# Two post-norm layers on one core: the router's transposes of six batches taken off TensorE

## The chip, the cores and the metric

The kernel runs on one core of a Trainium2 chip. The metric is the device time of one execution in microseconds, given as the median of several runs. Besides the times there is one profiled execution of the same program, recorded by the hardware profiler; all durations of single instructions come from it.

## What is computed

Eight batches of 512 tokens, each a row of 512 numbers in f32, go through two layers. Each layer is attention and then a feed-forward part, each of which is added to its input and followed by a layernorm. Cut to what matters:

```python
# layer 0, attention: 16 heads of 32, causal
q, k, v = x @ WQ.T + bq, x @ WK.T + bk, x @ WV.T + bv
attn = softmax(where(causal, -inf, q @ k.T / sqrt(32)))
x = layernorm(x + (attn @ v) @ WO.T + bo)
# layer 0, feed-forward: 8 experts, the best two for each token
logits = x @ (gate_weight + 2 * lora_B @ lora_A).T          # 512 -> 8
w, chosen = top_k(softmax(logits), 2);  w = w / w.sum()
x = layernorm(x + sum(w * expert_e(x) for e in chosen))
# layer 1: attention with 8 heads of 64, then a feed-forward part with integer weights (512 -> 1408 -> 512)
```

The change concerns one step of layer 0: how the rows `x` after the first layernorm are turned (features on the partitions, tokens along the row), so that TensorE can form `logits` from them.

## The kernel before

The whole of layer 0's attention is `attention0` (from L1182). It works batch by batch (b = 0 to 7), in each batch through four groups of four heads (g = 0 to 3), and in each group through three **units** (u = 0, 1, 2), which cover the key tiles 0, then 1 and 3, then 2. A place in this order is written (g, u) here. A unit does the following on TensorE: the scores of its own heads (`scores`, L1324), then whatever other work the plan has put into that place, then the product of the *unit before it* with the values (`product`, L1348), and in the units with u = 1 the row sums of the group before (`normalise`, `rs`, L1363). Between a unit's scores and its product lie ScalarE's exponential (L1328) and GpSimd's causal mask (L1333). VectorE adds up the exponentials (L1356), inverts the row sums (L1366) and scales (L1367).

`plan(b)` (from L1378) writes by hand which other work goes into which place: the values, queries and keys (the query and key of the next group, and those of the next batch's first group at the end), and the late work of the batch before it, pb = b - 1. For pb that work is, in order:

- `project(pb, t)`, four token tiles t: 8 matmul instructions of the output projection (L1276), VectorE adds the residual (L1277) and takes the statistics; after the last tile `layernorm` (L173 to L188) has GpSimd form the reciprocal deviation (L182, L183), VectorE normalise the four tiles (L185) and SyncE's queue write the rows to memory (L188);
- `turn(pb, c)`, four feature chunks c: four transposes on TensorE into one bank of PSUM (L1288) and a copy to `x1T` by VectorE (L194) or ScalarE (L192);
- `score(pb)`: eight matmul instructions give the logits (L491), ScalarE copies them (L1298); `choose(pb)`: four small pairs of matmuls (L503), then some 25 short VectorE instructions, which pick the experts;
- two batches later `dispatch`, `one_hot` and `enter`, which put the tokens into the experts' tables (L547 to L590).

`merge` (L776 to L794) adds a low-rank term to two chunks of the experts' weights: two pairs of matmuls (L781), two ScalarE scalings (L792), two GpSimd additions (L794).

TensorE's results other than scores and products share two PSUM banks (tag `mm`). `x1T` shares one room with the one-hot rows; `aoT`, the attention output, has one room, so that the first group's result of batch b can't be written before pb's last projection has read the old one; `r_inv` and the scaled merge rows share two rooms.

The order in `plan` isn't the final order. Outside of a few stretches marked `in_order`, a planner at build time lists each engine's instructions by its own estimate of when their inputs are ready, with the program's order as priority. Each engine, and SyncE's queue of DMAs, then works through its list strictly in order. So a lower-priority transfer may stand ahead of its place in the program: the input of batch b + 2 (`load_xT`, L1212) is issued in batch b as soon as `key(b, 3)` has read its room.

The class `Turn` (L73 to L104) is in the kernel already and serves the last feed-forward part (`IntegerFfn.blocks`, seven batches). It turns a batch without TensorE: VectorE transposes blocks of 32x32 (L88), four DMAs write each partition quarter's blocks to their place in memory (`out`, L93, 256 KB each), and one DMA of 1 MB reads the turned batch back (`back`, L96). The tokens then stand in the order (block of 32, tile, token), and `by_tile` puts them back into tile order at some later copy.

Of the kernel before, what the change touches and what calls it, by code (L numbers as in the profile page):

```python
# [9 lines left out]
F32 = mybir.dt.float32  # L10
# [8 lines left out]
P = 128  # L19
NB = 8  # L20
S = 512
D = 512
NT = S // P
ND = D // P
# [48 lines left out]
class Turn:  # L73
# [677 lines left out]
class Experts:  # L751
# [430 lines left out]
def attention0(env, guard, keep, routes, experts, dram, p_mm, tiles_ctx):  # L1182
# [4 lines left out]
    tc, nc, ins, xs, vec = env.tc, env.nc, env.ins, env.xs, env.vec  # L1187
# [3 lines left out]
    with ExitStack() as phase:  # L1191
        work = phase.enter_context(tc.tile_pool(name="a_work", bufs=1))
# [54 lines left out]
        def mm(shape, name):  # L1247
            return p_mm.tile(shape, F32, tag="mm", name=name)

        def value(b, t):  # L1250
            ps = mm([P, D], "ps_v")
            for c in range(ND):
                nc.tensor.matmul(ps, lhsT=xts[b][:, c, ts(t, P)], rhs=wv[:, c, :], start=c == 0, stop=c == ND - 1)  # L1253
            vs[t] = own.tile([P, D], F32, tag=f"v{t}", name=f"v{t}")
            nc.vector.tensor_tensor(vs[t], ps, row[:, 0, :], ALU.add)  # L1255

        def query(b, g):
            ps = mm([P, S], "ps_q")
            for c in range(ND):
                nc.tensor.matmul(ps, lhsT=wq[:, g, ts(c, P)], rhs=xts[b][:, c, :], start=c == 0, stop=c == ND - 1)  # L1260
            q = own.tile([P, S], F32, tag="q", name="q", bufs=2)
            nc.vector.tensor_scalar(q, ps, vec[:, V_BQ + g : V_BQ + g + 1], None, ALU.add)
            heads[b, g] = [q]

        def key(b, g):
            ps = mm([P, S], "ps_k")
            for c in range(ND):
                nc.tensor.matmul(ps, lhsT=wk[:, g, ts(c, P)], rhs=xts[b][:, c, :], start=c == 0, stop=c == ND - 1)
# [12 lines left out]
        x1Ts, logits = {}, {}  # L1281

        def turn(b, c):
            if c == 0:
                x1Ts[b] = work.tile([P, ND, S], F32, tag="x1T", name="x1T")
            ps = mm([P, S], "ps_x1T")
            for t in range(NT):
                nc.tensor.transpose(ps[:, ts(t, P)], xs[b][:, t, ts(c, P)], env.ident)  # L1288
            if b == NB - 2:
                nc.scalar.copy(x1Ts[b][:, c, :], ps)  # L1290
            else:
                env.evacuate(c, x1Ts[b][:, c, :], ps)

        def score(b):
            ps = mm([P, S], "ps_logits")
            router.logits(x1Ts.pop(b), ps)
            logits[b] = work.tile([P, S], F32, tag="logits", name="logits")
            nc.scalar.copy(logits[b], ps)  # L1298

        def choose(b):  # L1300
# [7 lines left out]
        def one_hot(b, places):  # L1308
            if places[0] == 0:
                rooms[b] = work.tile([P, ND, S], F32, tag="x1T", name="one_hot")  # L1310
            return router.one_hot(b, rooms[b], places)

        def enter(rows):
            router.enter(mm([P, 2, E * E_TILES], "ps_table"), *rows)

        def scores(b, g, u):
            q, k = heads[b, g]
            sc = p_sc.tile([P, 4, S], F32, tag="sc", name="sc")
            width = 0
            for kt in UNITS[u]:  # L1320
                w = S - P * kt
                for j in range(4):
                    hs = slice(HD * j, HD * (j + 1))
                    nc.tensor.matmul(sc[:, j, width : width + w], lhsT=k[hs, ts(kt, P)], rhs=q[hs, P * kt :],  # L1324
                                     start=True, stop=True)
                width += w
            p = own.tile([P, 4, width], F32, tag=f"p{u}", name="p", bufs=2 if u == 0 else 1)
            nc.scalar.activation(p, sc[:, :, :width], AF.Exp, scale=scale)  # L1328
# [49 lines left out]
        def plan(b):  # L1378

            todo = {(g, u): [] for g in range(ND) for u in range(len(UNITS))}  # L1380
            for slot, places in (((0, 0), (0, 1)), ((0, 1), (3,)), ((0, 2), (2,))):
                todo[slot] += [lambda t=t: value(b, t) for t in places]
            for g in range(ND):
                nb, ng = (b, g + 1) if g + 1 < ND else (b + 1, 0)
                if nb < NB:
                    todo[g, 1].append(lambda nb=nb, ng=ng: query(nb, ng))
                    todo[g, 2].append(lambda nb=nb, ng=ng: key(nb, ng))
            pb, last = b - 1, b == NB - 1
            if b:
                places = ((1, 0), (1, 0), (1, 1), (1, 1) if last else (1, 2))  # L1390
                for t, slot in enumerate(places):
                    todo[slot].append(lambda t=t: project(pb, t))
                places = ((2, 0),) * 4 if last else ((2, 1), (2, 1), (2, 2), (2, 2))
                for c, slot in enumerate(places):
                    todo[slot].append(lambda c=c: turn(pb, c))
                todo[(2, 1) if last else (3, 0)].append(lambda: score(pb))
                todo[(2, 2) if last else (3, 1)].append(lambda: choose(pb))
                if not last:
                    todo[2, 0].append(merge)
                    todo[3, 0].append(merge)  # L1400
# [34 lines left out]
        for b in range(NB):  # L1435
            todo = plan(b)
            for g in range(ND):
# [16 lines left out]
                for u in range(len(UNITS)):  # L1454
                    p = scores(b, g, u)
# [15 lines left out]
        b = NB - 1  # L1471
# [627 lines left out]
```

## Time and profile before

| | us |
|---|---|
| median of three runs (lowest, highest) | 2272.99 (2271.68, 2275.99) |
| the profiled execution's own time | 2270.12 |
| its span, first to last instruction | 2268.4 |
| TensorE busy in the span | 2224.5 |
| VectorE, ScalarE, GpSimd busy | 1257.6, 645.4, 494.5 |
| one batch of layer 0's attention, three stretches of 93, 94, 93 us: TensorE busy | 92.4, 92.8, 91.9 |
| the same: VectorE busy | 47.7, 60.9, 59.0 |

The span is cut into stages that follow one another: layer 0's attention to about 750 us, its experts to about 1210 us, layer 1's attention to about 1763 us and its feed-forward part to the end. A line of the timeline gives the start, the length, the engine, the line of the kernel, the operation, what it writes and reads, the tile shape, how many instructions were merged into it, and in brackets the idle time before it and what ended that. One f32 product of TensorE is two matmul instructions in these lines. The granted clock of TensorE is full (0.996) in the mean.

### The profile page before, as it was taken

The numbers are of one execution on the slowest core, as the hardware profiler recorded it, in microseconds if no ns is written. First come the engines' busy times: TensorE is split into PE (matmuls) and PEld (weight loads), VectorE is DVE, ScalarE is ACT, GpSimd is POOL, SyncE is SP. The second block draws the span as 40 slices with busy tenths as digits, with TensorE's granted clock in tenths as the row PEclk, the third lists the DMA queues.
The fourth block names the chain that finished last, engine by engine and source line by source line (L and its number), as shares of the span: only waits on it lengthen the run. The fifth ranks groups of instructions, "written<-read, shape, count | busy, mean of one in ns | idle before, by whom it ended". The sixth has DMA issues, their size and how long they took to land. (4 is left out here: it accounts for less than half of the span.)

```text
span 2268.4 us, 24071 instructions
## 1 busy us (share of the span) xinstructions
PE 2224.5 (98%) x9318; PEld 1142.3 (50%) x9318; DVE 1257.6 (55%) x2004; ACT 645.4 (28%) x937; POOL 494.5 (22%) x489
## 2 busy tenths in 40 slices
PE   9999999999999999999999999999999999999997
PEld 3344444444444444444453333433443778888876
DVE  3557676575767443242216776787666654445443
ACT  2332323323233221111124333332332222222222
POOL 2332423313223341131105223312211000000000
PEclk9999999999999999999999999999999999999999
DMA  8010101101022225242214111101100331111000
GB/s 292 19 56 1 56 19 38 57 1 56 28 64 75 93 66 194 88 125 88 89 58 160 34 56 56 47 10 47 38 0 1 103 93 56 56 56 46 29 19 20
DMA packets 74236, 141.31 MB, mean 62 GB/s; under 512 B 6770, under 2 KB 21106, under 8 KB 73218
## 3 DMA queue, kind: packets, MB, share of 16 engines
q1 hardware_dynamic: 62832, 104.01, 13.6%
q0 software_dynamic: 10560, 34.61, 5.4%
q8 instruction: 76, 1.25, 0.2%
q10 hardware_dynamic: 722, 1.07, 0.1%
q14 instruction: 46, 0.38, 0.1%
HBM read 96.93 MB, written 42.73 MB: 62 GB/s over the span
## 5 line engine op out<-in xcount | busy, mean ns | idle before, releaser
L877 PE MATMUL ps_gu<-experts,xrT 128*128 128x512 f32 (+1 forms) x520 | 247.1, 598 | 0.0
L1328 ACT ACTIVATE p<-sc 128x2048 f32<-128x2048 f32 (+1 forms) x96 | 152.9, 1592 | 189.0 <-PE sc L1324 182.2
L1333 POOL TENSOR_SCALAR_AFFINE_SELECT p<-p 128x512 f32<-128x512 f32 x128 | 91.8, 731 | 381.7 <-ACT p L1328 378.2
L1116 DVE SCALAR_TENSOR_TENSOR hT<-ps_u,vec,sg 128x512 f32<-128x512 f32 x88 | 65.5, 745 | 195.3 <-PE ps_u L1111 195.3
L1127 PE MATMUL ps_f<-ffn_w,h_half 128*128 128x512 f32 x672 | 170.3, 393 | 0.6 <-issue 0.4
L966 POOL TENSOR_TENSOR g_total<-g_total,r_inv 128x512 f32<-128x512 f32 x64 | 89.6, 1401 | 359.5 <-DVE r_inv L1677 283.5
L1677 DVE RECIPROCAL r_inv<-r_inv 128x512 f32<-128x512 f32 x32 | 106.9, 3339 | 97.6 <-ACT r_inv L963 97.6
L1647 ACT ACTIVATE p<-sc 128x1024 f32<-128x1024 f32 x128 | 124.0, 1021 | 125.9 <-PE sc L1644 125.9
L1356 DVE TENSOR_TENSOR p<-p 128x1536 f32<-128x1536 f32 (+2 forms) x96 | 129.1, 1345 | 39.5 <-POOL p L1333 22.5
L1127 PEld LDWEIGHTS ps_f<-ffn_w,h_half 128*128 128x128 f32 x672 | 124.4, 188 | 33.0 <-DVE h_half L1122 5.5
L880 DVE TENSOR_TENSOR h<-ps_gu,h 128x256 f32<-128x256 f32 x67 | 28.3, 423 | 202.5 <-ACT h L879 202.5
L1111 PE MATMUL ps_g<-x_high,ffn_w 128*128 128x512 f32 x352 | 138.9, 395 | 0.8 <-DVE x L1618 0.8
L1111 PE MATMUL ps_g<-x_low,ffn_w 128*128 128x512 f32 x352 | 139.0, 395 | 0.0
L1111 PE MATMUL ps_u<-x_low,ffn_w 128*128 128x512 f32 x352 | 138.7, 394 | 0.0
L1111 PE MATMUL ps_u<-x_high,ffn_w 128*128 128x512 f32 x352 | 138.7, 394 | 0.0
L894 PE MATMUL ps_y<-experts,hT 128*128 128x512 f32 (+1 forms) x272 | 127.9, 593 | 0.5 <-ACT hT L888 0.5
L1644 PE MATMUL sc<-qT,kT 64*128 64x512 f32 x512 | 127.3, 615 | 1.0 <-ACT qT L1565 0.7
L1260 PE MATMUL ps_q<-experts 128*128 128x512 f32 x256 | 121.1, 615 | 4.4 <-DMA experts<-in_xT 4.4
L1666 PE MATMUL av<-p,v 128*64 128x512 f32 x512 | 123.8, 605 | 0.0
L877 PEld LDWEIGHTS ps_gu<-experts,xrT 128*128 128x128 f32 x520 | 89.2, 191 | 67.6 <-issue 67.6
L1253 PE MATMUL ps_v<-experts 128*128 128x512 f32 x256 | 116.3, 602 | 3.2 <-DVE v L1255 3.2
L1612 PE MATMUL ps_o<-attn_out,aoT 128*128 128x512 f32 x256 | 117.3, 602 | 0.8 <-ACT r_inv L963 0.8
(259 smaller groups left out, 3521.5 us busy)
## 6 DMA issues: line engine op xcount, KB each, us to landing
results<-y SPq DMA_DIRECT2D x68, 256.0 KB, 2.0
x<-in_x SPq DMA_DIRECT2D x8, 1024.0 KB, 7.7
experts<-in_gate_up SPq DMA_DIRECT2D x8, 1024.0 KB, 10.7
rows<-x SPq DMA_DIRECT2D x32, 256.0 KB, 2.0
x<-rows SPq DMA_DIRECT2D x8, 1024.0 KB, 10.9
experts<-in_xT SPq DMA_DIRECT2D x7, 1024.0 KB, 5.4
turned<-turned SPq DMA_DIRECT2D x28, 256.0 KB, 3.9
turned<-turned SPq DMA_DIRECT2D x7, 1024.0 KB, 4.8
```

The source lines that it names most:

```text
L877: mm = nc.tensor.matmul(ps, lhsT=xT[:, c, :], rhs=self.weights(i, c), start=c == 0, stop=c == ND - 1)
L894: self.nc.tensor.matmul(ps, lhsT=hT[:, c, :], rhs=self.weights(i, ND + c), start=c == 0, stop=c == self.NI - 1)
L1111: nc.tensor.matmul(ps, lhsT=w[:, ts(dc, P)], rhs=x[:, dc, :], start=(dc, i) == (0, 0), stop=(dc, i) == (ND - 1, 1))
L1127: self.nc.tensor.matmul(os[t], lhsT=h[:, ts(t, P)], rhs=self.weights(2 * NHID + c), start=(c, i) == (0, 0), stop=(c, i) == (NHID - 1, 1))
L1253: nc.tensor.matmul(ps, lhsT=xts[b][:, c, ts(t, P)], rhs=wv[:, c, :], start=c == 0, stop=c == ND - 1)
L1260: nc.tensor.matmul(ps, lhsT=wq[:, g, ts(c, P)], rhs=xts[b][:, c, :], start=c == 0, stop=c == ND - 1)
L1328: nc.scalar.activation(p, sc[:, :, :width], AF.Exp, scale=scale)
L1356: nc.vector.tensor_tensor(total[:, :, P * kt :], total[:, :, P * kt :], p[:, :, at : at + w], ALU.add)
L1612: nc.tensor.matmul(ps, lhsT=state[b]["aoT"][:, c, ts(t, P)], rhs=w_out[:, c, :], start=c == 0, stop=c == ND - 1)
L1644: nc.tensor.matmul(sc[:, j, :], lhsT=st["kT"][hs, ts(kt, P)], rhs=st["qT"][g][hs, :], start=True, stop=True)
L1647: nc.scalar.activation(p, sc, AF.Exp, scale=scale)
L1666: nc.tensor.matmul(st["av"][HD * j : HD * (j + 1), :], lhsT=st["v"][:, kt, HD * j : HD * (j + 1)], rhs=p[:, j, :], start=kt == 0, stop=kt ...
```

## The change

For the batches 0 to 5 the four `turn` calls are replaced by one `blocks(b)`: four VectorE block transposes, four DMAs out and one back, with a new `Turn` and its own DRAM tile. The logits of these batches have their tokens in block order; ScalarE's copy to `logits` reads and writes through `by_tile` and restores tile order. The batches 6 and 7 are turned on TensorE as before.

While such a batch is the batch before (b = 1 to 6), the plan of b is another:

| place | before | after |
|---|---|---|
| (1,0) | project 0, 1 | project 0 |
| (1,1) | query, project 2, table | query, project 1, table |
| (1,2) | key, project 3 | key, project 2 |
| (2,0) | merge | project 3 |
| (2,1) | query, turn 0, 1 | query, blocks, merge |
| (2,2) | key, turn 2, 3 | key |
| (3,0) | score, merge | query of the next batch |
| (3,1) | query of the next batch, choose | score, merge |
| (3,2) | key of the next batch | key of the next batch, choose |

```diff
+        by_blocks = NB - 2
+        turns = Turn(env, dram, NT, "turned0")
+
+        def room(b):
+            x1Ts[b] = work.tile([P, ND, S], F32, tag="x1T", name="x1T")
+
+        def blocks(b):
+            room(b)
+            flat = x1Ts[b].rearrange("p k s -> p (k s)")
+            for t in range(NT):
+                turns.blocks(flat, t, xs[b][:, t, :])
+            turns.out(flat)
+            turns.back(flat)
+
...
-            nc.scalar.copy(logits[b], ps)
+            if b < by_blocks:
+                nc.scalar.copy(turns.by_tile(logits[b], False), turns.by_tile(ps, True))
+            else:
+                nc.scalar.copy(logits[b], ps)
...
+            pb, last = b - 1, b == NB - 1
+            by_dma = 0 <= pb < by_blocks
...
-                    todo[g, 1].append(lambda nb=nb, ng=ng: query(nb, ng))
+                    todo[g, 0 if by_dma and ng == 0 else 1].append(lambda nb=nb, ng=ng: query(nb, ng))
...
-                places = ((1, 0), (1, 0), (1, 1), (1, 1) if last else (1, 2))
+                places = ((1, 0), (1, 1), (1, 2), (2, 0)) if by_dma else ((1, 0), (1, 0), (1, 1), (1, 1) if last else (1, 2))
...
-                places = ((2, 0),) * 4 if last else ((2, 1), (2, 1), (2, 2), (2, 2))
-                for c, slot in enumerate(places):
-                    todo[slot].append(lambda c=c: turn(pb, c))
-                todo[(2, 1) if last else (3, 0)].append(lambda: score(pb))
-                todo[(2, 2) if last else (3, 1)].append(lambda: choose(pb))
+                if by_dma:
+                    todo[2, 1].append(lambda: blocks(pb))
+                else:
+                    for c in range(ND):
+                        todo[2, 0].append(lambda c=c: turn(pb, c))
+                todo[(3, 1) if by_dma else (2, 1)].append(lambda: score(pb))
+                todo[(3, 2) if by_dma else (2, 2)].append(lambda: choose(pb))
                 if not last:
-                    todo[2, 0].append(merge)
-                    todo[3, 0].append(merge)
+                    todo[2, 1].append(merge)
+                    todo[3, 1].append(merge)
```

More of the change, by code (lines that the diff above doesn't have):

```diff
@@ L1281, in attention0 @@
         x1Ts, logits = {}, {}
+        by_blocks = NB - 2
[9 more added lines that the diff above has]
+            turns.back(flat)
         def turn(b, c):
             if c == 0:
-                x1Ts[b] = work.tile([P, ND, S], F32, tag="x1T", name="x1T")
+                room(b)
             ps = mm([P, S], "ps_x1T")
@@ L1385, in plan @@
                 if nb < NB:
-                    todo[g, 1].append(lambda nb=nb, ng=ng: query(nb, ng))
+                    todo[g, 0 if by_dma and ng == 0 else 1].append(lambda nb=nb, ng=ng: query(nb, ng))
                     todo[g, 2].append(lambda nb=nb, ng=ng: key(nb, ng))
-            pb, last = b - 1, b == NB - 1
             if b:
-                places = ((1, 0), (1, 0), (1, 1), (1, 1) if last else (1, 2))
+                places = ((1, 0), (1, 1), (1, 2), (2, 0)) if by_dma else ((1, 0), (1, 0), (1, 1), (1, 1) if last else (1, 2))
                 for t, slot in enumerate(places):
                     todo[slot].append(lambda t=t: project(pb, t))
-                places = ((2, 0),) * 4 if last else ((2, 1), (2, 1), (2, 2), (2, 2))
-                for c, slot in enumerate(places):
-                    todo[slot].append(lambda c=c: turn(pb, c))
-                todo[(2, 1) if last else (3, 0)].append(lambda: score(pb))
-                todo[(2, 2) if last else (3, 1)].append(lambda: choose(pb))
+                if by_dma:
[5 more added lines that the diff above has]
+                todo[(3, 2) if by_dma else (2, 2)].append(lambda: choose(pb))
                 if not last:
-                    todo[2, 0].append(merge)
-                    todo[3, 0].append(merge)
+                    todo[2, 1].append(merge)
+                    todo[3, 1].append(merge)
             if b == 0:
```

## The prediction

> **What bounds the kernel now.** I read the busy shares first, then the chain that ended last, then one batch of layer 0 on TensorE's timeline.
>
> ```profile
> PE 2224.5 (98%) x9318; PEld 1142.3 (50%) x9318; DVE 1257.6 (55%) x2004; ACT 645.4 (28%) x937; POOL 494.5 (22%) x489
> ```
>
> TensorE is busy 98% of the span, and the chain that ended last is mostly TensorE, so time taken off TensorE's list is time won, as long as nothing else is late in its place. The two pairs of transposes and their surroundings in batch 4 (places (2,0) to (3,0)) show what they cost; the columns are start, length, line and what was written:
>
> ```profile
> 419.30 1.14 PE L1324 MATMUL sc<-q,k 32*128 32x512 f32 x8
> 420.28 1.03 PE L781 MATMUL ps_lora<-lora 16*128 16x512 f32 x4
> 421.23 0.64 PE L1348 MATMUL av<-p,v 128*32 128x256 f32 x8
> 422.44 1.15 PE L1324 MATMUL sc<-q,k 32*128 32x384 f32 x16 [0.57 <-ACT p L1328]
> 423.52 3.70 PE L1260 MATMUL ps_q<-experts 128*128 128x512 f32 x8
> 427.05 0.60 PE L1288 MATMUL ps_x1T<-ident,x 128*128 128x128 f32 x4
> 427.58 1.04 PE L1348 MATMUL av<-p,v 128*32 128x512 f32 x2
> 428.56 0.66 PE L1288 MATMUL ps_x1T<-ident,x 128*128 128x128 f32 x4
> ...
> 431.00 0.71 PE L1324 MATMUL sc<-q,k 32*128 32x256 f32 x8
> 431.64 3.70 PE L1268 MATMUL ps_k<-experts 128*128 128x512 f32 x8
> 435.18 0.60 PE L1288 MATMUL ps_x1T<-ident,x 128*128 128x128 f32 x4
> 435.71 0.83 PE L1348 MATMUL av<-p,v 128*32 128x384 f32 x2
> 436.47 0.66 PE L1288 MATMUL ps_x1T<-ident,x 128*128 128x128 f32 x4
> ...
> 438.05 1.14 PE L1324 MATMUL sc<-q,k 32*128 32x512 f32 x8
> ```
>
> The reader is to see two things. The transposes stand inside the products (av), of which otherwise four run side by side; two are torn off and run alone (0.98 us for two instructions). And at 422.44 TensorE waits for the exponential, because (2,0) holds almost nothing.
>
> **What goes.** In (2,1), from the end of the query's issue to the next scores: 431.00 - 427.05 = 3.95 us. The same products and row sums without transposes, in (1,1) of this batch, take 410.59 - 408.74 = 1.85. Difference 2.10. In (2,2): 438.05 - 435.18 = 2.87, against 419.30 - 418.30 = 1.00 for the same products in (1,2). Difference 1.87. Together 3.97 a batch. The transposes' own share of it is 0.53 + 0.59 + 0.53 + 0.59 = 2.24. In (2,0) the gap ahead of the scores goes too, since a projection (3.5 us) now stands there and covers the exponential (1.88 us): from 421.23 to 422.44 is 1.21, of which (1,1)'s like product needs 0.57, so 0.64. The rest of the batch, all places from (1,0) to (3,2), lasts 65.07 us (390.14 to 455.21). Its pieces at their undisturbed lengths make 59.7 without transposes: scores, products and row sums 6.2 for each of three groups, six queries and keys at 3.53, four projections at 3.53, table 1.84, logits 1.0, two merges 2.0, choice 0.9. So at most 65.07 - 59.7 = 5.4 us can be won in a batch, and I can place 3.97 + 0.64 = 4.6 of it; the rest is a low-rank pair torn across scores in (3,0).
>
> A rule of the Trainium skill would make the gain larger. The trace has 272 ns as the duration of a transpose, but 0.109 us from one's start to the next. "TensorE: Matmul & The Clock Gate", part 4, gives about 275 ns for a transpose in a kernel; sixteen at that price would be an estimated 4.4 us a batch instead of 2.24. Here the trace agrees with the length and shows that it isn't the price.
>
> **What TensorE gets instead.** The matmuls of the logits, projections, merges and queries are the same ones in other places. New is that a merge in (2,1) needs both banks of tag mm between the query and the row sums, and in (3,1) after the logits. The pairs can be torn as the transposes were. Below: 0. Above: 2.10 in (2,1), the transposes' own price there, and 1.0 in (3,1) (a pair's length). I take 0.7 and 0.4, nearer to nothing, since a merge has two tiles to place and not sixteen instructions.
>
> **The wait that is added.** Logits now wait for VectorE and two rounds of DMA. The prices come from the same class in the last stage and from this stage's norm:
>
> ```profile
> DMA to landing us min/median/max: 3.0/4.1/5.0
> ...
> turned<-turned SPq DMA_DIRECT2D x7, 1024.0 KB, 4.8
> ```
>
> ```profile
> 422.12 4.14 DVE L185 TENSOR_SCALAR x<-x,mv,rstd 128x512 f32<-128x512 f32 x4 [1.48 <-POOL rstd L183]
> ```
>
> From the end of project 3 (418.30) to the first normalised tile's start is 3.8 us (residual, statistics, GpSimd's deviation; 422.12). Four tiles take 4.14 beside GpSimd's mask and merge, but 0.55 each, 2.2, elsewhere; the merge now comes later, so 3.1. The query's copy between them is 0.4 to 0.75, the four block transposes 2.5 (1789.21 to 1791.7 in the last stage, 0.67 each, overlapped). From there the first write is issued, the read back 6.6 us later (1791.72 to 1798.33), and it lands 4.9 us after that (1803.25): 11.5. SyncE's queue holds one more thing: the load of x (1 MB), which is free to go as soon as the blocks are read, and the planner will list it ahead of the read back, which must wait for the writes. Two such loads 1.8 us apart (435.37 and 437.16) landed after 5.4 and 6.7 us, so a load in front costs the one behind it some 1 us; I add 0.7. Sum: 3.8 + 3.1 + 0.4 + 2.5 + 11.5 + 0.7 = 22.0 us.
>
> What covers it: after project 3, TensorE has the product of (2,0) 0.57, then (2,1) scores 1.07, query 3.53, merge 1.0, product and row sums 1.85, then (2,2) 5.2 and (3,0) 5.2 (scores, a key or query of 3.53, products), then (3,1)'s scores 1.07: 19.5, with the torn merge 20.2. So logits stall TensorE for 22.0 - 20.2 = 1.8 us. Behind them in its list stand the merge, the product of (3,0) and the row sums, and ScalarE's logits copy. Would the planner move the logits back? GpSimd's addition to the next x (L1442) waits 3 us for its load in each of five batches (15.3 us in all), ahead of merge work that is ready at 442.0, 4.8 us after the load's issue at 437.16: the planner takes such a load as landed by then, and will believe that logits are ready in time. I take the wait as real. Bounds: none (all lengths at their short end, 20.8, beside a fully torn merge), and 7 us (normalising at 4.14, both 1 MB loads ahead of the read back at 3.3 each, which is what 6.7 + 1.8 - 5.4 says of the second's own transfer).
>
> **What lies beside other work.** VectorE gets four transposes (2.7) and loses two copies (1.35), at 59 of 93 us busy; ScalarE loses two copies. The logits copy with split rows has no row in this stage; between its 0.58 and twice that I take 0.58, since it moves the same 512 numbers a partition, and ScalarE is free. 2 MB more a batch against a DMA share of 10% are covered but for the queueing above. Choice moves from 8 us before the batch's end to the end, so its 25 VectorE instructions meet the next batch's values, where TensorE already waits for the copy of a value (1.39 us at 372.15). Below 0, above 1.4; I take 0.5. The next batch's query in (3,0) has its input long before: its load was issued a batch ahead.
>
> A rule of the skill speaks against the whole change. Here four writes in 512-byte pieces land within 6.5 us (1791.72 to 1798.19). "VectorE: DVE Perf Modes", section "The three transpose paths", calls a plain DMA that transposes by strides 19 times slower than the crossbar's, and its "Rules for kernel authors" leave 128x128 to TensorE; stretched like that, the estimate for a 4.9 us transfer is 90 us, far beyond any cover. The writes here move whole 512-byte runs, which is why I follow the rows.
>
> **The sum.** Per batch 5.4 - 0.7 - 0.4 - 1.8 - 0.5 = 2.0 us won; six batches 12 us. The profiled execution took 2270.1, so 2258; the median of the runs is 2.9 above it, so 2261 from there. I write 2260.
>
> **Rivals.**
> - *The planner places the logits late enough*, behind the merge, product and row sums of (3,1) (2.85 us of work): the stall of 1.8 is covered, and the merge ahead of them isn't torn. 5.4 - 0.7 - 0.5 = 4.2 a batch, 25 us: 2245 to 2248 (by the profiled execution, by the median), so 2246. For it: the planner does reorder by readiness. Against: its early GpSimd add. Chance 0.18.
> - *The road through memory is too long*: the key of (2,2) frees the next input's room at about 433, near the time at which the writes land, and that load, too, goes ahead of the read back. The stall then is about 6 us with slow normalising, and 5.4 - 1.6 - 6 = -2.2 a batch, 13 us more: 2284. It decides from a stall of 4 us on (5.4 - 0.7 - 0.4 - 0.5 is 3.8). For it: the queue is in order, and 11.5 us of its road has no slack. Against: the read back is listed earlier if the planner thinks the writes short. Chance 0.24.
> - *The change does what it says, but the stall and the choice eat the gain* (3 to 4 us): 2270. Chance 0.11.
> - The forecast, 2260: chance 0.47.
>
> **The numbers.** A difference under 0.2% (4.5 us) can't be told from no change in this kernel. The forecast's case is faster but for a small part (0.02 within), so faster 0.63, within 0.13, slower 0.24. The range reaches down to 2242, where nothing is torn and nothing waits but the choice (5.4 - 0.5 = 4.9, six times 29), and up to 2284, the slow rival.
>
> **What would show it.** TensorE at full clock with a batch of 89 to 92 us in place of 93.4; no L1288 in six batches; ahead of L491 a gap for the DMA of x1T of 1 to 3 us, in each of six batches; the read back landing about 12 us after the last block transpose, with x's load issued ahead of it; no gap ahead of the scores after (2,0). I am wrong if that gap is over 4 us, if TensorE stalls on the banks in (2,1) by more than a transpose pair did, or if VectorE runs late at the batch's start.

## The result, and the profile after

The changed kernel takes 2287.7 us (median of six runs, 2282.9 to 2289.2) against 2271.6 for the kernel before (six runs on the same chip, 2267.7 to 2276.0). The ratio is 1.0066, 95% interval 1.0054 to 1.0078: **slower by 16 us**. The forecast was 2260 and faster; its range ended at 2284.

The profiled execution took 2287.86 us, its span is 2286.1. The line of busy times in the page of the changed kernel:

```profile
PE 2237.0 (98%) x9222; PEld 1132.3 (50%) x9222; DVE 1259.6 (55%) x2016; ACT 640.0 (28%) x925; POOL 485.0 (21%) x489
```

The 96 transposes are gone from TensorE (9318 instructions became 9222), and yet TensorE is busy for 12.5 us longer. The mean granted clock fell from 0.996 to 0.989. So what is left got slower or stands more apart; and nearly all of it lies in the stage that was changed: the first write to `results` (start of the experts) moves from 748.66 to 765.41 us, by 16.75 of the 17.7 us that the span grew.

The nearest answer is in batch 4 again, places (2,0) to (3,1), on TensorE's timeline of the changed kernel (start, length, line, what was written, count, and in brackets the wait before it):

```profile
428.56 1.15 PE L1341 MATMUL sc<-q,k 32*128 32x384 f32 x16
429.63 3.70 PE L1260 MATMUL ps_q<-experts 128*128 128x512 f32 x8
433.27 1.12 PE L781 MATMUL ps_lora<-lora 16*128 16x512 f32 x2
434.32 1.04 PE L1365 MATMUL av<-p,v 128*32 128x512 f32 x2
437.45 1.12 PE L781 MATMUL ps_lora<-lora 16*128 16x512 f32 x2 [2.09 <-DVE q L1262]
438.50 0.63 PE L1365 MATMUL av<-p,v 128*32 128x512 f32 x3
...
438.98 2.42 PE L1380 MATMUL rs<-p,ones 128*32 128x512 f32 x7
441.32 1.24 PE L1341 MATMUL sc<-q,k 32*128 32x256 f32 x8
...
452.49 1.15 PE L1341 MATMUL sc<-q,k 32*128 32x384 f32 x16
453.57 1.06 PE L491 MATMUL ps_logits<-x1T,r_wr 128*32 128x512 f32 x8
454.56 1.12 PE L781 MATMUL ps_lora<-lora 16*128 16x512 f32 x2
455.62 1.04 PE L1365 MATMUL av<-p,v 128*32 128x512 f32 x2
456.59 1.12 PE L781 MATMUL ps_lora<-lora 16*128 16x512 f32 x2
```

The gap that was predicted ahead of the logits (L491) isn't there: they start right behind the scores. The gap is in (2,1), at 437.45: the second pair of the merge wants a bank of `mm`, and that bank still holds the query. VectorE's timeline of the same stretch says why:

```profile
431.81 2.56 DVE L185 TENSOR_SCALAR x<-x,mv,rstd 128x512 f32<-128x512 f32 x4 [1.48 <-POOL rstd L183]
434.29 2.48 DVE L88 STREAM_TRANSPOSE x1T<-x 128x512 f32<-128x512 f32 x4
436.69 0.70 DVE L1262 TENSOR_SCALAR q<-ps_q,vec 128x512 f32<-128x512 f32 x1
```

TensorE has issued the last of the query at about 433.2. VectorE's list has four normalisations and four block transposes ahead of its copy, so the copy starts 3.5 us later. The waits of the whole stage name the same pair, in each of the six batches (engine, line, releaser: total us, times, longest):

```profile
PE ps_lora L781 <- DVE q L1262: 12.5, 6, 2.1
```

What comes after the wait costs as much again. The busy times by stretch, TensorE's clock in the third column from the end:

```profile
437.00:439.00 2.00, 1.55 (x10) 0.49 (x13) 0.40 (x1) 0.33 (x1) 0.00 (x0) 1.00 0.43 84
439.00:441.00 2.00, 2.00 (x14) 0.28 (x6) 1.20 (x1) 0.27 (x1) 1.27 (x1) 0.58 0.91 169
441.00:443.00 2.00, 2.00 (x12) 0.91 (x10) 2.00 (x2) 1.06 (x3) 0.00 (x0) 0.57 0.95 220
443.00:445.00 2.00, 2.00 (x6) 0.92 (x5) 2.00 (x1) 0.65 (x1) 0.63 (x1) 1.00 0.96 219
```

At 0.58 and 0.57 over 4 us, the clock was halved for 3.4 us, which loses 1.7 us. Here seven instructions of the row sums last 2.42 us, where eight take 1.04 in place (1,1) of the same batch (413.61). Most of the loss is therefore counted as TensorE busy: in the whole span TensorE is idle for only 5.2 us more than before (49.1 against 43.9).

The queue of DMAs in that batch, from SyncE's timeline (issue, time the issue took, line):

```profile
436.79 3.79 SPq L93 DMA_DIRECT2D turned<-x1T  x4
440.75 1.25 SPq L1216 DMA_DIRECT2D x<-in_x  x1
444.29 0.33 SPq L96 DMA_DIRECT2D x1T<-turned  x1
```

The next x is loaded ahead of the read back, as predicted. From the first write's issue to the read back's it takes 7.5 us; the read back lands 7.6 us later, at 451.9. From the end of the last projection (427.9) the road is 24.0 us long.

The table counts a place from its first score to the next place's, in us, as the mean of the batches 2 to 5. Other places are within 0.1 of each other in all kernels but for (1,0), which is 5.27 with the new plan and 8.70 with the old.

| kernel | (0,0) | (0,1) | (0,2) | (2,0) | (2,1) | (2,2) | (3,0) | (3,1) | (3,2) | batch | median us |
|---|---|---|---|---|---|---|---|---|---|---|---|
| before | 8.70 | 10.68 | 9.07 | 3.14 | 8.56 | 7.06 | 3.69 | 8.20 | 5.28 | 93.5 | 2271.6 |
| after | 8.70 | 10.00 | 9.07 | 5.27 | 13.08 | 6.00 | 5.27 | 7.00 | 6.07 | 96.2 | 2287.7 |
| e1 | 8.83 | 10.00 | 9.07 | 6.32 | 7.41 | 6.70 | 7.92 | 4.19 | 6.07 | 92.2 | 2265.5 |
| e2 | 8.71 | 10.00 | 9.07 | 5.27 | 11.33 | 7.06 | 5.27 | 7.00 | 6.25 | 95.7 | 2288.0 |
| e3 | 8.70 | 10.00 | 9.07 | 5.27 | 8.46 | 5.28 | 5.27 | 14.35 | 6.38 | 98.5 | 2303.1 |
| e4 | 9.49 | 10.00 | 9.07 | 6.32 | 7.41 | 6.70 | 5.27 | 4.75 | 8.29 | 93.0 | 2267.2 |
| e5 | 9.41 | 10.00 | 9.07 | 5.27 | 8.46 | 5.28 | 5.27 | 9.25 | 7.89 | 95.6 | 2284.5 |
| e6 | 12.35 | 10.00 | 9.07 | 6.32 | 7.41 | 5.28 | 7.92 | 3.79 | 6.53 | 94.4 | 2278.1 |
| e7 | 9.54 | 10.00 | 9.07 | 6.32 | 10.13 | 7.06 | 7.92 | 3.79 | 6.07 | 95.6 | 2285.8 |
| e8 | 8.70 | 10.00 | 9.07 | 3.14 | 6.56 | 5.28 | 3.14 | 20.64 | 5.28 | 101.0 | 2314.6 |
| e9 | 9.49 | 10.00 | 9.07 | 6.32 | 7.41 | 7.17 | 5.27 | 11.54 | 5.28 | 97.3 | 2293.8 |
| e11 | 8.70 | 10.00 | 9.07 | 5.27 | 13.18 | 5.91 | 5.27 | 7.00 | 6.07 | 96.2 | 2287.4 |
| e12 | 9.49 | 10.00 | 9.07 | 6.32 | 10.20 | 7.06 | 6.88 | 8.88 | 5.30 | 98.9 | 2308.4 |
| e13 | 9.50 | 10.00 | 10.41 | 6.32 | 7.41 | 7.17 | 5.27 | 3.99 | 5.28 | 91.1 | 2253.8 |
| e14 | 9.49 | 10.00 | 10.41 | 6.32 | 10.20 | 7.06 | 6.88 | 3.99 | 5.28 | 95.3 | 2284.9 |
| e15 | 8.70 | 10.00 | 10.36 | 3.14 | 8.56 | 7.06 | 3.69 | 8.20 | 5.28 | 94.1 | 2274.9 |

After less before is 2.67 us a batch, 16.0 in six: (1,0) -3.4, (2,0) +2.1, (2,1) +4.5, (2,2) -1.1, (3,0) +1.6, (3,1) -1.2, (3,2) +0.8, (0,1) -0.7.

### The profile page after: what moved, and what is told of

It is laid out like the page before. It is cut to its first block, busy times and chain, and to the rows that moved or that the text cites. A ratio compares the mean times of both kernels' runs of the same rounds, so it can differ in the third digit from the quotient of the medians.

```text
span 2286.1 us, 23911 instructions
## 1 busy us (share of the span) xinstructions
PE 2237.0 (98%) x9222; PEld 1132.3 (50%) x9222; DVE 1259.6 (55%) x2016; ACT 640.0 (28%) x925; POOL 485.0 (21%) x489
## 3 DMA queue, kind: packets, MB, share of 16 engines
q10 hardware_dynamic: 722, 1.07, 0.1%
## 5 line engine op out<-in xcount | busy, mean ns | idle before, releaser
L1373 DVE TENSOR_TENSOR p<-p 128x1536 f32<-128x1536 f32 (+2 forms) x96 | 136.3, 1420 | 60.8 <-PE av L1365 59.2
L1350 POOL TENSOR_SCALAR_AFFINE_SELECT p<-p 128x512 f32<-128x512 f32 x128 | 82.7, 658 | 404.9 <-ACT p L1345 338.4
L1268 PE MATMUL ps_k<-experts 128*128 128x512 f32 x256 | 118.3, 605 | 0.2 <-ACT r_inv L963 0.2
## 6 DMA issues: line engine op xcount, KB each, us to landing
experts<-in_gate_up SPq DMA_DIRECT2D x8, 1024.0 KB, 11.3
```

The source lines that it names most:

```text
L1373: nc.vector.tensor_tensor(total[:, :, P * kt :], total[:, :, P * kt :], p[:, :, at : at + w], ALU.add)
```

## The experiments

The first theory was that the place of the merges costs the time: with VectorE late, the merge in (2,1) waits for its bank. The rivals were the road through memory, the choice at the batch's start, and the block copy.

**e1: the merges back in (2,0) and (3,0), all else as changed.**

```diff
-                    todo[2, 1].append(merge)
-                    todo[3, 1].append(merge)
+                    todo[2, 0].append(merge)
+                    todo[3, 0].append(merge)
```

> The changed kernel with its two merges back in (2,0) and (3,0); nothing else moved. Theory A (the loss is the banks: in (2,1) the second merge pair waits for a bank that VectorE empties only after four normalised tiles and four block transposes): no wait of a merge pair for VectorE's query copy is left, (2,1) lasts about 6.5 us instead of 12.8, and if nothing else is short, 4 to 4.5 us a batch are won against the kernel before: about 2246 us. Theory B (the road through memory is too long for the cover, and in the changed kernel the bank wait only hid that): the turned rows land 24 us after project 3's end, as in the changed kernel, but logits come up after 20.5 us; TensorE waits 3 to 4 us for that DMA in each of six batches and loses up to 2 us more to the lowered clock after it: 2268 to 2278 us.

Measured: 2265.5 us, ratio to before 0.9971 (0.9961 to 0.9982): 22 us less than the changed kernel, and faster than before. Place (2,1) falls from 13.1 to 7.4. VectorE is as late as in the changed kernel; TensorE now meets the uncopied query one place later. TensorE's timeline of e1, batch 4:

```profile
428.37 3.70 PE L1268 MATMUL ps_k<-experts 128*128 128x512 f32 x8 [1.35 <-DVE q L1262]
...
437.70 1.12 PE L781 MATMUL ps_lora<-lora 16*128 16x512 f32 x2
438.75 0.62 PE L1365 MATMUL av<-p,v 128*32 128x256 f32 x2
439.30 1.12 PE L781 MATMUL ps_lora<-lora 16*128 16x512 f32 x2
440.35 0.63 PE L1365 MATMUL av<-p,v 128*32 128x256 f32 x6
440.91 1.15 PE L1341 MATMUL sc<-q,k 32*128 32x384 f32 x16
```

A wait of 1.35 us is left, and behind it the clock isn't halved: the granted clock is 1.00 in every stretch from 420 to 460. The merge in (3,0) is torn all the same ((3,0) takes 7.92, its pieces 6.2). So the merge's place decides the sign in this kernel. The time lies between what the two theories gave (2246, and 2268 to 2278): the late copy costs less here, but it still costs.

**e2: the new places, and all batches turned on TensorE.** The blocks and their DMAs are out; `turn` stands in (2,1) and (2,2) as before.

```diff
-                    todo[2, 1].append(lambda: blocks(pb))
+                    for c, slot in enumerate(((2, 1), (2, 1), (2, 2), (2, 2))):
+                        todo[slot].append(lambda c=c: turn(pb, c))
```

> The changed kernel's places for projections, query, merges, logits and choice, but with the rows turned on TensorE (two chunks in (2,1), two in (2,2)) for all batches, no block transposes and no DMA round. Theory A: (2,1) is still crowded (query, eight transposes, a merge, row sums on two banks), so it stays slow even without block transposes, by 2 to 4 us a batch: 2278 to 2295 us. Theory C (the block transposes and their DMAs are what costs; the places alone are harmless): within 6 us of the kernel before, 2266 to 2278 us. Theory B says nothing of it.

Measured: 2288.0, ratio 1.007 (1.0053 to 1.0087), the same as the changed kernel. The places alone cost the whole 16 us, and in them the turning off TensorE earns nothing: (2,1) takes 11.3 instead of 13.1, (2,2) 7.1 instead of 6.0. The waits of e2 show none for the query's copy; its (2,1) is long by torn groups, eight transposes and a merge among the products.

**e3: the query of (2,1) copied by ScalarE.** This takes the late copy away and leaves the merge where it is.

```diff
-            nc.vector.tensor_scalar(q, ps, vec[:, V_BQ + g : V_BQ + g + 1], None, ALU.add)
+            if g == ND - 1 and 1 <= b < NB - 1:
+                nc.scalar.activation(q, ps, AF.Identity, bias=vec[:, V_BQ + g : V_BQ + g + 1])
+            else:
+                nc.vector.tensor_scalar(q, ps, vec[:, V_BQ + g : V_BQ + g + 1], None, ALU.add)
```

> The changed kernel; only the copy of the last group's query of batches 1 to 6 out of PSUM is made by ScalarE instead of VectorE, so that its bank doesn't wait behind the norm and the block transposes. Theory A alone: the 2 us wait of the merge pair and the clock loss after it go, 4 to 5 us a batch, six batches: about 2260 us. Theory B: the logits come up that much sooner, ahead of the landing at 24 us after project 3, and TensorE waits there instead, 3 to 4 us with the clock loss again: 2278 to 2290 us.

Measured: 2303.1, ratio 1.0134 (1.0117 to 1.0151): slower still, and above what either theory gave (2290 at the most). The bank wait is gone and (2,1) falls to 8.5. But now TensorE arrives at the logits early. Its timeline in e3:

```profile
439.14 1.97 PE L781 MATMUL ps_lora<-lora 16*128 16x512 f32 x4
...
453.44 1.15 PE L1344 MATMUL sc<-q,k 32*128 32x384 f32 x16
459.28 1.93 PE L491 MATMUL ps_logits<-x1T,r_wr 128*32 128x512 f32 x8 [4.69 <-DMA x1T<-turned]
461.14 2.07 PE L781 MATMUL ps_lora<-lora 16*128 16x512 f32 x2
463.14 1.92 PE L1368 MATMUL av<-p,v 128*32 128x512 f32 x2
```

The merge in (2,1) is whole again (four instructions in 1.97 us). The wait for the read back is 4.69 us in this batch, 2.6 to 2.9 in the other five, and everything behind it runs at twice its length. The clock by stretches of e3:

```profile
460.00:462.00 2.00, 2.00 (x9) 0.50 (x2) 0.00 (x0) 0.59 (x1) 0.96 (x2) 0.50 0.04 14
...
466.00:470.00 4.00, 4.00 (x16) 0.58 (x14) 0.96 (x1) 0.60 (x1) 1.27 (x1) 0.50 0.00 0
```

Half clock for all of 460 to 470. So the second rival of the prediction, the road that is too long, was there under the bank's wait, which had hidden it in the changed kernel.

**e11: only the loads held.** The changed kernel, with the loads of the next x and of the input issued behind the read back.

```diff
-                    load_x(b + 1)
+                    with tc.issue_after(turns.read.ins) if 0 < b <= by_blocks else nullcontext():
+                        load_x(b + 1)
...
-                        load_xT(b + 1)
+                        with tc.issue_after(turns.read.ins) if b > 1 else nullcontext():
+                            load_xT(b + 1)
```

> The changed kernel with nothing but the two 1 MB loads held back behind the read of the turned rows. Theory A: the rows land some 3 us sooner and nothing follows, since in the changed kernel logits already come up 1.7 us after the landing, behind the bank wait: 2284 to 2290 us, as the changed kernel. If the landing bounded the changed kernel: 2275 or less. Rival D (the later x makes GpSimd's addition late, and the masks behind it): over 2292.

Measured: 2287.4, ratio 1.0071 (1.0056 to 1.0086), as the changed kernel. The read back's landing bounds nothing while the bank's wait stands.

**e5: e3 and the loads held** (both edits above).

> e3_query_scalar (query copy of (2,1) by ScalarE, merges in (2,1) and (3,1)), with one thing more: the 1 MB loads of x and of the input two batches ahead are held back in SyncE's queue until the read of the turned rows has been issued. Theory B, with the loads as the term that was sized too small (the read back takes 7.6 us to land in the changed kernel, 4.9 in the last stage where nothing is in front): it lands in about 5 us, the writes before it in 6.6, some 3.5 us sooner in all; the wait at the logits falls from 4 to 6 us to under 2, the clock after it stays up, and the time falls from 2303 to 2258-2275 us. If the writes and the read are slow of themselves in this stage (other traffic, the norm's rows), nothing lands sooner: 2295 us or more.

Measured: 2284.5, ratio 1.0056 (1.0039 to 1.0072): 19 us less than e3, so the two loads are a real term once TensorE waits for the read back. In e3 it took 7.1 us to land (median). In e5, by the ends of TensorE's waits, it takes 4.9 to 5.0 us in five batches and 7.5 in batch 4. TensorE's waits for it fall from 18.1 us in six batches to 6.8. The expected 2258 to 2275 wasn't reached: (3,1) still takes 9.25, and the choice's matmuls (L503) wait 9.1 us in five batches for ScalarE, behind its work on `r_inv`.

**e8: the plan before, and only the turning changed.** The projections, queries, merges, logits and choice keep the old places; `blocks` stands in (2,0). Against the kernel before, where that differs:

```diff
-                for c, slot in enumerate(places):
-                    todo[slot].append(lambda c=c: turn(pb, c))
+                    todo[2, 0].append(lambda: blocks(pb))
```

> The kernel before with nothing but the turning changed: block transposes and the DMA round in (2,0) for batches 0 to 5, all else in its old place, logits in (3,0). Theory B: from project 3 to the logits there are about 17 us of work, the rows land after 24 to 25: TensorE waits 7 us in each of six batches, and works at a lowered clock for some us after it, against 4 us won: 2300 to 2335 us. If the road were as short as in the last stage (22 us or less by the prediction's terms), the wait is under 5 us and the time within 2270 to 2295.

Measured: 2314.6, ratio 1.0185 (1.0168 to 1.0202). TensorE waits 25.4 us in five batches for the read back, 5.2 at the longest, and the mean clock is 0.975. Without new places the road through memory isn't covered: the places of the change are needed.

**e7: e2 with the merges back** (the edit of e1 on e2).

> e2_places_only (all batches turned on TensorE, no DMA round) with the merges back in (2,0) and (3,0); projections, queries, logits and choice stay in the new places. Theory A (it is the merges in (2,1) and (3,1) that cost, not the other moves): the whole 16 us go, 2264 to 2276 us. If the projection in (2,0), the query in (3,0) or the late choice cost by themselves: 2280 us or more.

Measured: 2285.8, ratio 1.006 (1.0044 to 1.0077). The first theory, in the form that the merges' place is what costs, falls here: with TensorE turning, the merges moved back save 2 us and not 16. (2,1) takes 10.1 us, 1.6 more than before: project 3 comes one place later, so the first four transposes meet rows that are still being normalised (1.2 us for them instead of 0.5), and a pair of the merge from (2,0) is torn across the scores (0.9). Beside e1, which has the same places and blocks, it says what the turning off TensorE is worth there: 2285.8 - 2265.5 = 20 us.

**e4: room for the logits.** Merges in (2,0) and (3,1), the logits one place later, the choice in the next batch.

```diff
-                todo[(3, 1) if by_dma else (2, 1)].append(lambda: score(pb))
-                todo[(3, 2) if by_dma else (2, 2)].append(lambda: choose(pb))
+                todo[(3, 2) if by_dma else (2, 1)].append(lambda: score(pb))
+                if b > 1:
+                    todo[0, 0].append(lambda: choose(b - 2))
...
-                    todo[2, 1].append(merge)
+                    todo[2, 0].append(merge)
```

> The changed kernel with merges in (2,0) and (3,1), logits in (3,2) after the next batch's key, and choice after the values of the next batch's (0,0). No merge shares (2,1) with the query, and logits come up about 26 us after project 3, later than the landing at 24. Theories A and B together: neither a bank wait nor a wait for the DMA is left, 3.5 to 5 us a batch are won: 2242 to 2252 us. Theory A without B, or B without A: the same. Theory C (block transposes on VectorE and the DMAs themselves are what costs), or a VectorE that runs late at the start of a batch: over 2265 us.

Measured: 2267.2, ratio 0.9981 (0.997 to 0.9991), short of the 2242 to 2252 expected. No wait for the DMA is left, but the key waits for the query's copy (8.3 us in six batches), the logits for ScalarE's `r_inv` (9.3) and the row sums for the scaled merge rows (4.4): `r_inv` and the merge's rows share two rooms, and the merge in (3,1) holds them until GpSimd has added them.

**e6: merges back, the query by ScalarE, and the loads held** (the edits of e1, e3 and e11).

> The changed kernel with its merges back in (2,0) and (3,0), the query copy of (2,1) by ScalarE, and the two loads behind the read back. Theories A and B together say that all three waits are gone (second merge pair and key for VectorE's copy, logits for the DMA, each under 1 us a batch): 2248 to 2260 us, faster than e1_merges_back (2265). If only the banks matter, no better than e1 less the 1.4 us a batch that the key waits there: 2257; if VectorE's extra work or the DMA traffic itself costs, no better than 2265.

Measured: 2278.1, ratio 1.0034 (1.0023 to 1.0045), well above the 2260 expected at most. Places (2,2) and (3,1) are as short as in any kernel, but (0,0) rises from 8.8 (e1) to 12.4. The load of x is later; GpSimd's addition to it (L1462 in the changed kernel) waits 3.7 us for it and takes 4.5, ahead of causal masks; VectorE waits up to 12.7 us for these, and is then late with the choice, behind whose first steps TensorE waits for its bank at the next values (11.3 us in five batches). The cost was moved, not removed.

**e9: all known waits removed by places.** Merges in (2,0) and (2,2), the query by ScalarE (e3's edit), the logits in (3,2), the choice in the next (0,0) (e4's).

```diff
-                    todo[2, 1].append(merge)
-                    todo[3, 1].append(merge)
+                    todo[2, 0].append(merge)
+                    todo[2, 2].append(merge)
```

> The changed kernel with merges in (2,0) and (2,2) (no row sums and no logits beside them), the query copy of (2,1) by ScalarE, logits in (3,2), choice after the values of the next batch's (0,0); the loads are not held back. Theories A and B: no merge is torn beside row sums, no key waits for VectorE, and logits come up over 27 us after project 3, after the rows landed: units add up to about 90 us a batch against 93.5 before: 2248 to 2256 us, the fastest so far. Rival D (GpSimd: the addition to the next x holds up the masks, and products wait for it, whatever the places): 2262 us or more.

Measured: 2293.8, ratio 1.0099 (1.0084 to 1.0115). One wait is left in the stage, and it is a new one. TensorE's timeline in e9, and GpSimd's:

```profile
450.89 1.15 PE L1344 MATMUL sc<-q,k 32*128 32x384 f32 x16
458.48 1.93 PE L1368 MATMUL av<-p,v 128*32 128x512 f32 x8 [6.44 <-POOL p L1353]
```

```profile
453.34 4.50 POOL L1468 TENSOR_TENSOR x<-x,row 128x2048 f32<-128x2048 f32 x1 [3.50 <-DMA x<-in_x]
457.79 1.80 POOL L1353 TENSOR_SCALAR_AFFINE_SELECT p<-p 128x512 f32<-128x512 f32 x3
```

GpSimd works its list in order. In the changed kernel the addition to the next x stands behind a mask of (3,0) (450.38 and 450.98); here it is listed ahead of it. It waits 3.5 us for its load and takes 4.5, and the masks that TensorE needs stand behind it. The merge has left (3,1), but that this is what moved the addition wasn't tested.

**e12: the places of e9, all turned on TensorE.**

> The places of e9_roomy_late, but all batches turned on TensorE (two chunks in (2,1), two in (2,2), with the merge). It says what taking the transposes off TensorE is worth where nothing waits: by the trace of before 2.2 to 4.0 us a batch, 13 to 24 us in all. Theories A and B: 2264 to 2278 us. If it is as fast as e9_roomy_late, the transposes were free on TensorE.

Measured: 2308.4, ratio 1.0161 (1.0147 to 1.0175), with the same wait for the masks (17.6 us in five batches): 14.5 us above e9, and outside of the 2264 to 2278 expected. The turning is worth something again, but both kernels are held by GpSimd.

**e13, e14, e15: GpSimd's addition held behind a mask of its own batch**, in e9, in e12 and in the kernel before (`masks` keeps each mask's instruction).

```diff
-                    nc.gpsimd.tensor_tensor(xs[b], xs[b], row[:, 1:2, :].to_broadcast([P, NT, D]), ALU.add)
+                    with tc.issue_after(masks[b, 0, 2].ins):
+                        nc.gpsimd.tensor_tensor(xs[b], xs[b], row[:, 1:2, :].to_broadcast([P, NT, D]), ALU.add)
```

> The plan with merges in (2,0) and (2,2), query copied by ScalarE, logits in (3,2) and the choice in the next batch's (0,0), blocks turned by VectorE and DMA, as before; new is only that GpSimd's addition to the next x is held behind the mask of (0,2) of its own batch, so that it can't stand ahead of the masks of (3,0). Theory (the addition is the whole of the loss): the masks come on time, the product in (3,1) no longer waits 6.4 us, place (3,1) falls from 11.5 to about 3.3 to 4.5 us, the batch to 89 to 91 us, the kernel to 2243 to 2256. Rival (the late places lose for another reason: the choice or the logits' bank in (3,2) and (0,0), or the held addition now delays the masks of (1,0)): 2262 to 2285.

> The same plan and the same hold, with all eight batches turned on TensorE. Theory: the wait of the products for GpSimd's masks goes as well, and what is left against the kernel with blocks is what the transposes cost in these places, 2.2 us (their own issue) to 4 us a batch in six batches: 13 to 24 us above the kernel with blocks, so 2258 to 2280. Rival: the wait is not the addition's, and it stays at 2295 to 2310.

> The kernel before with only GpSimd's addition held behind the mask of (0,2) of its own batch. Its TensorE is busy 98% and waits for no mask there, so theory: within 4 us of before, 2267 to 2276. Rival (the addition's place costs the kernel before too, by the merge rows that stand behind it): faster by 5 us or more; or slower by 5 us or more, if it now delays the masks of (1,0).

Measured: e13 2253.8 (2252.7 to 2254.4), ratio **0.9925** (0.9912 to 0.9939); e14 2284.9, 1.0063 (1.0049 to 1.0076); e15 2274.9, 1.002 (1.0011 to 1.0029). e13 is the fastest of all: 17 us less than before, 34 less than the changed kernel. The addition was the whole of e9's loss against what its places promised (2248 to 2256): (3,1) falls from 11.5 to 4.0, and the only wait of TensorE in the stage is 5.4 us in five batches, for VectorE at the ranks. TensorE in e13 at the same places as shown for e9 and for the changed kernel:

```profile
424.62 1.97 PE L781 MATMUL ps_lora<-lora 16*128 16x512 f32 x4
...
432.79 1.15 PE L1344 MATMUL sc<-q,k 32*128 32x384 f32 x16
433.87 1.06 PE L1370 MATMUL av<-p,v 128*32 128x512 f32 x8
434.75 1.04 PE L1385 MATMUL rs<-p,ones 128*32 128x512 f32 x8
...
440.20 1.06 PE L491 MATMUL ps_logits<-x1T,r_wr 128*32 128x512 f32 x8
```

The merge is whole, products and row sums run in eights, and the logits find their rows. At these places the turning off TensorE is worth 2284.9 - 2253.8 = 31 us, more than the 24 that e14's expectation allowed for. By the table it is 4.3 us a batch, 26 in six: 2.8 in (2,1), 1.6 in (3,0); the first write to `results` comes 27.5 us earlier (733.28 against 760.81), and the rest of the 31 isn't placed.

e15 is 4 us above before; the interval of its ratio leaves out 1 by little. It shows what the hold costs by itself: (0,2) takes 10.4 in place of 9.1 in all three kernels that have it. In e15 (0,1) gives 0.7 of it back.

## Why the prediction was wrong

**The gain: the transposes' share right, the whole too high.** 5.4 us a batch were to be won, from 65.1 down to 59.7 in the places (1,0) to (3,2). The changed kernel takes 68.4 there, e13 61.2, which is 3.9 less than before; but in e13 the choice stands in the next (0,0), which takes 0.8 more, so 3.1 of the 5.4 were had on like terms. The share of the turning was put at 3.97. With everything else in its old place (e8) the two places of the transposes fall by 2.0 and 1.8, 3.8 together, so that reading held; at other equal places the turning was worth 4.3 (e13 against e14), 3.4 (e1 against e7) and nothing (changed kernel against e2). (2,0) came out as priced: 5.27 where its pieces make 5.17, and the wait for the exponential is gone.

**The merge in (2,1): the step that failed.** "I take 0.7 and 0.4, nearer to nothing, since a merge has two tiles to place and not sixteen instructions." The number of instructions wasn't the measure. The merge's second pair needs the bank that the query holds, and that comes free only when VectorE copies the query. From the end of the query's issue (429.63 + 3.53 = 433.16) to the next scores (441.32) TensorE needed 8.2 us for work of 2.85 (merge 1.0, products and row sums 1.85): 5.3 us lost in that batch, 5.6 in the mean, eight times the price and nearly three times its upper bound. Of the 5.3, 2.1 are the wait, about 1.0 the halved clock (0.42 of 2 us and a part of the next stretch), and the rest, some 2.2, the torn pairs. Another 0.7 us of half clock falls into (2,2), which takes 6.0 where its pieces make 5.2. e1 takes this wait away and wins 22 us; e3 takes it away in another manner and (2,1) falls by 4.6.

The 1.0 that e3 leaves was mis-sized in the ideal sum. There a merge stood at 1.0, its length in (2,0) of the kernel before (four instructions in 1.03 us), where no query or key is ahead of it. Behind a query or key it takes 1.97 us even when ScalarE copies at once: in e13 that copy of the key ends at 425.42 and the merge's second pair starts at 425.47; in e3 the copy of the query ends at 439.93 and the pair starts at 439.98.

All that was needed to see it was in the prediction: it listed norm, query's copy and block transposes on VectorE in a row, but as a road for the rows, in which the copy cost "0.4" and stood ahead of the block transposes. In the changed kernel it stands behind them (436.69). The prediction didn't ask who waits for that copy. Its last sentence named this very case ("if TensorE stalls on the banks in (2,1) by more than a transpose pair did"), but gave it neither a price nor a rival.

**The merge in (3,1): 2.1 in place of 0.4.** Its pieces make 4.9 and it takes 7.0. It is torn as the transposes were, so here the upper bound of 1.0 was the nearer one, and even that was low.

**The stall at the logits: none in place of 1.8, by luck.** The road took 24.0 us, not 22.0: four writes 7.5 where the row gave 6.6, the read back 7.6 with x's load ahead of it where 4.9 + 0.7 was taken; the norm, at 2.56, was shorter than 3.1. The cover of 20.2 was right to 0.6 us: in e3, where nothing else stalls, TensorE goes from the end of project 3 (433.8) to the end of (3,1)'s scores (454.6) in 20.8 us, and then waits 4.7. In the changed kernel the lost time in (2,1) made TensorE later by more than that: it reached the logits at 453.57, the rows had landed at 451.9. So the second rival's mechanism was real, and it decides as soon as the merge is mended without giving the logits more room. e8 shows it with the old places.

**The choice: 0 in place of 0.5** in the changed kernel, where (0,0) didn't move and (0,1) fell by 0.7; its matmuls stand in (3,2) at the 0.8 to 0.9 that the pieces allowed. In e6 it cost up to 3.7 together with late masks, beyond the upper bound of 1.4.

**The sum.** Over the nine places, 5.4 of ideal gain less 6.4 for (2,1) and (2,2), 2.1 for (3,1) and 0.3 of small rests is -3.4; with the 0.7 won in (0,1) it is -2.7 a batch, which is what the table shows.

**Open.** That the wait is what halves the clock, and not the thin stretch of torn pairs around it, wasn't separated. Nor were the 5 us of e14's distance from e13 placed that lie outside the table's places. Between e13 and the ideal sum without the choice (58.8) are 2.4 us a batch: about 1.0 is the merge behind the key in (2,2), 1.1 lie in (2,0) and (2,1), where a pair of the other merge is torn across the scores, and 0.3 are not placed.

## What to carry to other kernels

When a step is moved on the engine that sets the time, ask of each bank it needs which engine empties it, and what stands ahead of that emptying in that engine's list; a copy that is cheap as a term of its own may be the one for which the bound engine waits. Price a wait of a busy TensorE with what follows it, torn groups and a lower clock, and remove one wait at a time with the next one in view: here the bank, the DMA and GpSimd's list hid one another, and some repairs taken alone (e3, e11) looked like failures. A change that earns nothing may still be right where it is paired with the right places: the turning alone (e8) and e13's plan without the turning (e14) both lost, and together (e13) they won 17 us.

## What the runs showed of the hardware

**The clock was halved after waits of 2 us, but not after every one.** In the changed kernel each of the six waits of 2.1 us was followed by 3.41 us at half clock, in one batch by 6.83; in e3 the wait of 4.7 us went with 13.65. Behind the waits of 1.35 to 1.5 us in e1 the clock stayed full. The length alone doesn't decide: it also stayed full behind 2.6 us in two batches of e6 and behind 3.0 us in one of e12, while in another batch of e6 it fell after 1.4 us. In layer 0's attention every stretch at half clock lasts 3.41 us or a multiple of it, up to 17.07 (e8). The Trainium skill, "TensorE: Matmul & The Clock Gate", section "HAM oscillation — how this bites in real kernels", puts the rule at idle gaps above about 3.4 us; in these runs the clock also fell after shorter gaps, and the measurement decides.

**GpSimd's large addition stops VectorE's additions.** In e13 the addition to x runs from 464.08 to 468.59 us. On VectorE's timeline the additions of exponentials around it are:

```profile
442.03 0.62 DVE L1378 TENSOR_TENSOR p<-p 128x512 f32<-128x512 f32 x1
...
465.83 3.31 DVE L1378 TENSOR_TENSOR p<-p 128x512 f32<-128x512 f32 x1
```

The same instruction takes 3.31 us instead of 0.62, and ends 0.55 us after GpSimd does, as if it had begun only then. The batches 1 to 7 of e13 all show it, with 3.25 to 3.31 us. The query's copy out of PSUM beside the same addition isn't held: in the changed kernel it takes 0.75 us at 452.03, with the addition running from 450.98 to 455.51. Of the 1.3 us in (0,2) that the hold costs, 1.07 are TensorE's wait at the ranks for VectorE, which is late behind that row. The Trainium skill, "SBUF — State Buffer", section "SBUF: two separate sides", describes such a lock between a VectorE operation with two inputs in SBUF and one of GpSimd that reads SBUF; this row agrees.

**The queue's order has a price.** A read back of 1 MB lands after 7.1 us (median) with the 1 MB load of x issued ahead of it and the input's right behind (e3). With both behind it (e5) TensorE could go on after 4.9 to 5.0 us in five batches and 7.5 in the sixth.
